# Mixture of experts at the end of a one-core Trainium2 kernel: the table of experts' results laid out by choice, partition and tile, and half-block copies in the last two pairs

## The chip, the cores and the metric

The kernel runs as one program on one core of a Trainium2 chip. The metric is the device time of the whole program in microseconds (us). It computes four layers of attention and feed-forward on the same tokens; the change concerns the last feed-forward layer, a mixture of 64 experts, and above all the last 50 us of the program.

## The reference, cut to what matters

1024 tokens (4 x 256) of width 256. Seven earlier blocks update `x`; the eighth is this one:

```python
def _L3_ffn_ref(hidden_states, gate_w, gate_proj_w, up_proj_w, down_proj_w):
    B, S, H, I, E, K = (2, 128, 256, 96, 64, 8)
    x = hidden_states.reshape(-1, h)
    router_logits = x @ gate_w
    routing_weights, selected = jax.lax.top_k(router_logits, K)
    routing_weights = jax.nn.softmax(routing_weights, axis=-1)
    ...                                   # the 8192 (token, expert) rows sorted by expert
    gate = jax.lax.ragged_dot(hidden_sorted, gate_proj_w, group_sizes)
    up = jax.lax.ragged_dot(hidden_sorted, up_proj_w, group_sizes)
    down = jax.lax.ragged_dot(jax.nn.silu(gate) * up, down_proj_w, group_sizes)
    out = down[unsort].reshape(-1, K, h)
    out = jnp.sum(out * routing_weights[..., None], axis=1)
    return out.reshape(b, s, h)
x = x + _L3_ffn_ref(_layernorm(x), ...)
```

Each token goes to 8 of 64 experts; the 8 results are weighted, summed and added to `x`.

## The kernel before

**Tokens and tiles.** The 1024 tokens are NT = 8 tiles of 128 (P) partitions: token number = tile t x 128 + partition p. Each token has K3 = 8 choices j. Choices are numbered in the order of the experts, so choice 0 of a token is its lowest-numbered expert and choice 7 its highest.

**Tables in device memory.** `hs` holds the experts' inputs: 192 (CAP) rows for each expert. A row is 256 values and one further column, which holds the number of the row of `yd` to which the result belongs. That number is written by the `iota` in `normed_rows` (L1674); unused rows of `hs` hold a number past the end, and the scatter skips them. `yd` has 8192 rows of 256 floats (1 KB each), one for each token and choice: row = token x 8 + choice.

**The experts' loop** (`experts`, L2040) takes two experts (a pair) in each of 32 steps p. Step p computes the gate and up products of pair p (`ps_gu` L2055, `upper_sums` L1982) and the down products of pair p - 1 (`main_sums` L1996, `rest_sums` L2002). The down result `y` has three blocks of 128 rows. Blocks 0 and 2 are complete after `main_sums`; block 1 is half of one expert and half of the other and is made by `rest_sums`. ScalarE copies all three blocks from PSUM to the row buffer `hb` in one instruction (L2083); in the step after the last pair it copies blocks 0 and 2 first (L2079) and block 1 later (L2088). `put_results` (L2007) then has GpSimd issue three indirect DMAs (one for each block, order 0, 2, 1) that scatter the rows to `yd`.

**Loads of results.** `load_results` (L1908) is called from `beside` once all experts that can hold a choice are through: choices 0 and 1 after pair 23, choice 2 after pair 27, 3 after 28, 4 after 29, 5 after 30, and 6 with 7 after pair 31. The SyncE queue (SP) issues these loads in program order, and each waits for the landing of the puts of all pairs up to its own. There are twelve loads, 8 MB in all:

| choices | loads x size | contiguous run in `yd` | order inside a load |
|---|---|---|---|
| 0 and 1 | 2 x 1 MB (tiles 0-3, tiles 4-7) | 2 KB | both choices of a token |
| 2; 3 | 1 x 1 MB each | 1 KB | one choice of all tokens |
| 4; 5 | 2 x 512 KB each (tiles 0-3, 4-7) | 1 KB | one choice |
| 6 and 7 | 4 x 512 KB (two tiles each) | 2 KB | both choices of a token |

The destinations are `deep` and `wt` (choices 0 to 3), `q` and `wmask` (4, 5), `cx` and `ctxT` (6, 7).

**The weighted sums** (`sums`, L2094). Even tiles are summed on TensorE with diagonal weights (`sum_result` L1944), odd tiles on VectorE by multiply-adds into `x` (`add_result` L1939). Four of the VectorE adds are placed beside the last pairs. The other twenty, of choices 1 to 5, wait for `tick`, a GpSimd memset that stands behind the last put (L2101). Then for t = 0, 2, 4, 6: sums of choices 6 and 7 of tile t on TensorE, two adds of tile t + 1 on VectorE, the store of tile t + 1, `add_to_x` of tile t on VectorE (L1779), and its store. The stores go out on ScalarE's queue (L2096).

In this part of the program the order of instructions on each engine is the order written; no scheduler moves them.

Of the kernel before, what the change touches and what calls it, by code (L numbers as in the profile page):

```python
# [23 lines left out]
I32 = mybir.dt.int32  # L24
# [4 lines left out]
P = 128  # L29
B, S, D = 4, 256, 256  # L30
NTOK = B * S
NT = NTOK // P
# [14 lines left out]
E3, I3, K3 = 64, 96, 8  # L47
# [7 lines left out]
LOADS = ((0, 1), (2,), (3,), (4,), (5,), (6, 7))  # L55
# [3 lines left out]
RPP = 2 * CAP // P  # L59
# [57 lines left out]
class Flow:  # L117
# [117 lines left out]
def model(ctx: ExitStack, tc: tile.TileContext, a: dict, out: bass.AP):  # L235
    nc = tc.nc
# [14 lines left out]
    def held(pool, shape, name, dtype=F32):  # L251
        return pool.tile(shape, dtype, tag=name, name=name)
# [4 lines left out]
    def x_t(t):  # L257
        return xb[t // 2][:, t % 2, :]
# [21 lines left out]
    yd = dram.tile([NPAIR, D], F32, tag="yd", name="yd")  # L280

    ctxT = held(early, [P, 2, NTOK], "ctxT")
    cx = held(early, [P, NT, D], "cx")
# [39 lines left out]
        channel_multiplier=-1,  # L323
# [126 lines left out]
    def layers(nk):  # L450
# [41 lines left out]
        def sc(name):  # L492
            return ("sc", [P, 16], name)
# [859 lines left out]
        before = [len(js) for js in puts]  # L1353
# [317 lines left out]
        def normed_rows(t, hx, rows, row_data):  # L1671

            yield Op(POOL, 0.2, (), (hx,))
            nc.gpsimd.iota(  # L1674
                rows[:, :, D : D + 1].bitcast(I32), pattern=[[1, K3], [0, 1]], base=t * P * K3,
                channel_multiplier=K3,
            )
            s = yield Op(DVE, 0.7, (X[t],), new=[sc("st")])
            nc.vector.bn_stats(s[:, 0:6], x_t(t))
            nc.vector.bn_aggr(s[:, 6:8], s[:, 0:6])  # L1680
            nc.vector.tensor_scalar(s[:, 7:8], s[:, 7:8], LN_EPS, None, ALU.add)
            rstd = rstds[:, t : t + 1]
            yield Op(POOL, 0.75, (s,), (s,))
            nc.gpsimd.tensor_tensor(rstd, s[:, 7:8], mhalf, ALU.pow)
            nc.gpsimd.tensor_scalar(s[:, 8:9], s[:, 6:7], rstd, -1.0, ALU.mult, ALU.mult)
            for k in range(2):
                yield Op(ACT, 0.93, (X[t], s, hx), (row_data[k],))
                j = slice(k * K3 // 2, (k + 1) * K3 // 2)
                nc.scalar.activation(
                    rows[:, j, :D], x_t(t).unsqueeze(1).to_broadcast([P, K3 // 2, D]), AF.Identity,  # L1690
                    bias=s[:, 8:9], scale=rstd,
                )
            release(s)
            hx.ready = hx.used = row_data[1].ready
# [131 lines left out]
    with tc.If(rv > 0):  # L1826
# [7 lines left out]
        for t in range(NT):  # L1834
            h = layernorm(t, moe, 1)
# [4 lines left out]
        with tc.For_i(0, E3, 1) as e:  # L1840
# [4 lines left out]
            for c in range(NCH):  # L1845
                pg, pu = ps_mm([I3, CH], "ps_g3"), ps_mm([I3, CH], "ps_u3")
                for ps, o in ((pg, 0), (pu[HALF:], I3), (pu[:HALF], P)):
                    for dc in range(2):
                        at = dc * 2 * I3 + o
# [16 lines left out]
    backs, gats = [], {}  # L1866
    late_rows = [q.bitcast(F32)[:, : NT // 2 * D] for q in (*q2, wmask.rearrange("p t s -> p (t s)"))]
    free_homes = [homes[k % WEIGHTS] for k in range(E3 // GROUP - FIRST, E3 // GROUP - FIRST + 4)]
    n_pairs = E3 // 2

    def choice_weights(t):
# [8 lines left out]
    hbTs, acts, gs = (  # L1880
        [moe_tile(shape, f"{name}{k}", 1) for k in range(2)]
        for name, shape in (
            ("hbT", [P, 2, RPP * P]), ("act", [I3, 2, CAP]), ("g4", [I3, 2, CAP])
        )
    )
# [21 lines left out]

    def load_results(js, p):  # L1908

        half = NT // 2  # L1910
        for h in range(2):
            if js[0] in (0, 2, 3) and (h == 0 or js[0] == 0):
                g = free_homes.pop(0)[:, : NT * D]
            elif js[0] in (4, 5):
                g = late_rows[2 * (js[0] - 4) + h]
            elif js[0] == 6:
                g = (cx.rearrange("p t d -> p (t d)"), ctxT.rearrange("p c r -> p (c r)"))[h]
            else:
                continue
            g = g.rearrange("p (t j d) -> p t j d", j=len(js), d=D)  # L1920
            n = 2 if js[0] == 6 else g.shape[1]
            for j in js:
                gats.setdefault(j, []).append(g)
            for t0 in range(0, g.shape[1], n):
                at = (h * half + t0) * P * K3
                source = yd[at : at + n * P * K3, :].rearrange("(t p j) d -> p t j d", p=P, j=K3)
                ld = nc.sync.dma_start(
                    g[:, t0 : t0 + n].rearrange("p t j d -> p t (j d)"),
                    source[:, :, js[0] : js[-1] + 1, :].rearrange("p t j d -> p t (j d)"),
                )  # L1930
                needs(ld, "back", backs[: RPP * (p + 1)], "results of these choices alone")

    def result(t, j):
        gs = gats[j]
        n = NT // len(gs)
        return gs[t // n][:, t % n, j - min(js for js in LOADS if j in js)[0], :]

    def add_result(t, j):
        return nc.vector.scalar_tensor_tensor(  # L1939
# [56 lines left out]
    def main_sums(act, dn):  # L1996
        y = ps_acc([P, 4, D], "ps_y")
        for i in range(2):
            nc.tensor.matmul(y[:, 2 * i], act[:, i, whole[i]], dn[:, i], start=True, stop=True)  # L1999
        return y  # L2000
# [39 lines left out]
    def experts():  # L2040
        for p in range(in_early - 1, AHEAD - 1):
            load_rows(p)

        nc.scalar.activation(silu, mhalf, AF.Silu)
        nc.vector.tensor_mul(lgs, lgs, wide(kept))
        hbT, turned = rows_turned(0)
        before = ready = None
        for p in range(n_pairs + 1):
            if p < n_pairs:
                e = 2 * p % GROUP  # L2050
                gu, dn = (v[:, e : e + 2] for v in weights[2 * p // GROUP])
                ps = ps_mm([P, 2, CAP], "ps_gu")
                for i in range(2):
                    for dc in range(2):
                        nc.tensor.matmul(  # L2055
                            ps[:, i], gu[:, i, dc, :P], hbT[:, dc, mine[i]], start=dc == 0, stop=dc == 1
                        )
                g = gs[p % 2]
                gated = nc.scalar.activation(g, ps[:I3], AF.Silu)  # L2059
                tc.declare_no_dep(gated.ins, group="gated", reason="ordered through the sums before")  # L2060
                tc.add_to_no_dep_group("gated", gated.ins)
                own = hbT
                act = acts[p % 2]
                if p == 0:
                    ready = upper_sums(p, own, gu, g, act)
                turned = None
                if p + 1 < n_pairs:
                    hbT, turned = rows_turned(p + 1)
                    if p > 0:
                        known(turned, ready)  # L2070
                half = nc.vector.tensor_mul(act[HALF:], ps[I3:], g[HALF:])  # L2071
                product_made(p, half)
            if p > 0:
                yb = hbs[p - 1][:, :, :D]
                y = main_sums(*before)
                if p < n_pairs:
                    ready = upper_sums(p, own, gu, g, act)
                else:
                    nc.scalar.copy(yb[:, ::2, :], y[:, :RPP:2])  # L2079
                mm = rest_sums(y, *before)  # L2080
                if p < n_pairs:
                    known(mm, half)
                    copied = nc.scalar.copy(yb, y[:, :RPP])  # L2083
                    for group in ("back", "rows", "results"):
                        tc.declare_no_dep(copied.ins, group=group, reason="ordered through the rows' use")
                    tc.add_to_no_dep_group("results", copied.ins)
                else:
                    nc.scalar.copy(yb[:, 1, :], y[:, 1])  # L2088
                put_results(p - 1, yb)
                beside(p - 1)  # L2090
            if p < n_pairs:
                before = act, dn
# [120 lines left out]
```

## Time and profile before

| | us |
|---|---|
| median of 4 runs (lowest to highest) | 642.49 (641.33 to 645.07) |
| the profiled execution, its own time | 643.27 |
| its span, first to last instruction | 641.5 |
| mean granted TensorE clock | 0.973 |

| engine | busy us (share of the span) |
|---|---|
| TensorE (PE) | 588.6 (92%) |
| VectorE (DVE) | 424.2 (66%) |
| ScalarE (ACT) | 373.8 (58%) |
| GpSimd (POOL) | 404.0 (63%) |

The experts' loop lies at about 482 to 617 us of the span and what follows it at 617 to 641.5. Times of instructions below are counted from the start of the span. In the lines of a timeline the columns are start, duration (for merged lines, from the first start to the last end), engine, source line, operation, output <- input, count, and in brackets the idle time of the engine before it and what ended it. POOLq, SPq and ACTq are the sequencers of those engines, which issue DMAs. Shares over the whole span say little about this change; it is read from its last 50 us.

### The profile page before, as it was taken

Reading aid. Unit: us, or ns where it says so; the run is one execution under the profiler, and the core shown is the slowest. Engines: PE = TensorE matmul, PEld = TensorE weight load, DVE = VectorE, ACT = ScalarE, POOL = GpSimd, SP = SyncE. Lnnn points to the kernel's source line nnn. Section 1 sums busy time; section 2 is a strip of 40 time slices with the busy share of each in tenths; the row PEclk is TensorE's granted clock in tenths of the full one; section 3 lists DMA queues with packets and bytes.
Section 4 is the critical chain, followed back from the end, with each engine's and each line's share of the span. In section 5 each row is a group of like instructions: output and inputs, shape, how many; then the busy total and the mean of one; then the engine's idle time right before and its main releaser. Section 6 shows DMA issues by size and latency. Waiting matters only on the chain.

```text
span 641.5 us, 10891 instructions
## 1 busy us (share of the span) xinstructions
PE 588.6 (92%) x3727; PEld 450.6 (70%) x3740; DVE 424.2 (66%) x1063; ACT 373.8 (58%) x900; POOL 404.0 (63%) x532
## 2 busy tenths in 40 slices
PE   5997699998999999999999989999739999999995
PEld 4774357686688777877877866886527788778873
DVE  5779947777787789569978757475434555433437
ACT  2233338768888966456886678679434454445420
POOL 6998897132726544664735875787773777676660
PEclk9999899998999999999999989999959999999998
DMA  8999999820210023000003111053458878979687
GB/s 279 363 387 249 212 208 190 269 72 2 83 33 3 1 66 115 2 0 1 1 2 107 42 67 53 31 193 108 156 175 294 263 233 275 308 227 310 211 266 262
DMA packets 66304, 98.12 MB, mean 153 GB/s; under 512 B 7206, under 2 KB 54007, under 8 KB 66240
## 3 DMA queue, kind: packets, MB, share of 16 engines
q1 hardware_dynamic: 56320, 78.40, 42.4%
q0 software_dynamic: 7680, 16.84, 7.4%
q10 hardware_dynamic: 2240, 2.10, 1.0%
q8 instruction: 31, 0.51, 0.4%
q14 instruction: 33, 0.27, 0.1%
HBM read 58.42 MB, written 43.07 MB: 158 GB/s over the span
## 4 chain that ended last, share of the span: by engine, by line
PE 57%; DVE 11%; POOL 10%; ACT 9%; issue 6%; DMA 5%; POOLq 0%; DVEq 0%; SPq 0%; ACTq 0%
PE ps_gu L2055 6%; PE ps_q L1519 5%; PE ps_y L1623 3%; POOL yd L2009 3%; PE ps_u L1986 3%; PE ps_y L1999 3%; PE tp_hb L1892 3%; PE ps_y L1402 2%; POOL hs L1702 2%; PE ps_p L742 2%; PE ps_u L1604 2%; DMA hs<-hx,slots 2%; PE ps_u L1120 2%; PE ps_s L1380 2%; PE tp_q L1277 2%
## 5 line engine op out<-in xcount | busy, mean ns | idle before, releaser
L2009 POOL DMA_INDIRECT yd<-hb x84 | 84.1, 1001 | 34.2 <-issue 20.1
L1702 POOL DMA_INDIRECT hs<-hx,slots x64 | 65.7, 1027 | 24.2 <-issue 13.0
L903 POOL TENSOR_TENSOR st<-st,mhalf 128x1 f32<-128x1 f32 x56 | 33.0, 594 | 57.5 <-DVE st L899 43.5
L1566 ACT ACTIVATE e<-ps_s,nm 128x128 f32<-128x128 f32 x128 | 45.8, 412 | 5.6 <-DVE nm L1560 5.5
L1991 DVE TENSOR_TENSOR act<-ps_u,g 64x192 f32<-64x192 f32 x64 | 22.6, 354 | 39.7 <-PE ps_u L1986 39.3
L2083 ACT COPY hb<-ps_y 128x768 f32<-128x768 f32 x27 | 21.6, 800 | 36.4 <-PE ps_y L2004 36.4
L2071 DVE TENSOR_TENSOR act<-ps_gu,g 32x384 f32<-32x384 f32 x32 | 18.0, 562 | 34.0 <-ACT g L2059 33.8
L1478 POOL TENSOR_TENSOR hh<-g,v 128x512 f32<-128x512 f32 x16 | 20.2, 1273 | 23.8 <-ACT g L1476 20.0
L1281 ACT ACTIVATE qT<-tp_q,rnd 128x512 bf16<-128x512 f32 (+2 forms) x48 | 25.7, 567 | 12.5 <-PE tp_q L1277 12.4
L1566 ACT ACTIVATION_READ_ACCUMULATOR e<-ps_s,nm 128x1 f32 x128 | 31.2, 252 | 0.0
L1533 POOL TENSOR_TENSOR deep<-rt 64x512 f32<-64x512 f32 x20 | 27.3, 1364 | 5.3 <-DVE rt L1529 2.7
L1519 PE MATMUL ps_q<-qc,deep 96*128 96x256 f32 x128 | 30.4, 381 | 0.0
L906 DVE TENSOR_SCALAR h<-x,st 128x256 f32<-128x256 f32 x56 | 27.0, 494 | 5.1 <-POOL st L903 4.8
L1185 ACT ACTIVATE e<-ps_s,nb 128x256 f32<-128x256 f32 x64 | 30.1, 493 | 0.0
L1623 PE MATMUL ps_y<-bo,u 128*128 128x256 f32 x128 | 29.5, 383 | 0.1
L2059 ACT ACTIVATE g<-ps_gu 96x384 f32<-96x384 f32 x32 | 15.6, 486 | 23.2 <-PE ps_gu L2055 23.2
L1900 ACT COPY hbT<-tp_hb 128x768 f32<-128x768 f32 x31 | 24.7, 798 | 7.1 <-PE tp_hb L1892 7.1
L1529 DVE TENSOR_TENSOR rt<-ps_q,rope 128x512 f32<-128x512 f32 x32 | 20.9, 684 | 9.4 <-PE ps_q L1519 9.4
L1583 DVE TENSOR_TENSOR e<-e,nm 128x512 f32<-128x512 f32 x32 | 25.8, 806 | 1.3
L1519 PEld LDWEIGHTS ps_q<-qc,deep 96*128 96x128 f32 x128 | 24.1, 190 | 3.4 <-ACT qc L1505 0.3
L1623 PEld LDWEIGHTS ps_y<-bo,u 128*128 128x128 f32 x128 | 24.0, 193 | 3.4 <-ACT u L1608 0.5
L1120 PE MATMUL ps_g<-hT,w_gate 128*128 128x512 bf16 x69 | 18.6, 406 | 8.3 <-ACT hT L1100 4.5
(373 smaller groups left out, 1778.8 us busy)
## 6 DMA issues: line engine op xcount, KB each, us to landing
hs<-order SPq DMA_DIRECT2D x1, 12336.0 KB
hb<-hs SPq DMA_DIRECT2D x28, 385.5 KB, 5.3
yd<-order SPq DMA_DIRECT2D x1, 8192.0 KB, 31.0
deep<-in_w_gu SPq DMA_DIRECT2D x8, 768.0 KB, 5.8
wt<-in_w_gu SPq DMA_DIRECT2D x6, 768.0 KB, 7.6
deep<-in_w_dn SPq DMA_DIRECT2D x8, 384.0 KB, 6.8
wt<-yd SPq DMA_DIRECT2D x3, 1024.0 KB, 7.1
wt<-in_w_dn SPq DMA_DIRECT2D x6, 384.0 KB, 9.5
```

The costliest lines, as they stand in the source:

```text
L903: nc.gpsimd.tensor_tensor(s[:, 8:9], s[:, 7:8], mhalf, ALU.pow)
L906: nc.vector.tensor_scalar(h[:, k, :], x_t(t), ss[k][:, 6:7], ss[k][:, 8:9], ALU.subtract, ALU.mult)
L1120: nc.tensor.matmul(ps.ap, w[:, dc, o : o + P], q[:, dc, :], start=k == 0, stop=k == n - 1)
L1185: nc.scalar.activation(e[:, mt, :], s[:, mt, :], AF.Exp, bias=nb[:, mt : mt + 1], accum_out=tot[:, 2 * j + mt : 2 * j + mt + 1],)
L1519: nc.tensor.matmul(ps.ap[:, k, :], w[:, hp * P : (hp + 1) * P], qc.ap, start=True, stop=True)
L1533: nc.gpsimd.tensor_add(qv(q[i])[r, hps, :], t0[r], t1[r])
L1566: nc.scalar.activation(wide[:, k, :], s.ap[:, k, :], AF.Exp, bias=nm[:, k : k + 1], accum_out=tot[:, k : k + 1],)
L1583: nc.vector.tensor_mul(wide, wide, tot.unsqueeze(2).to_broadcast([P, n, nk * P]))
L1623: nc.tensor.matmul(y.ap, u[:, hp, :], bo3[:, hp, :], start=hp == 0, stop=hp == H3 // 2 - 1)
L1702: put = nc.gpsimd.indirect_dma_start(out=hs[:, :], out_offset=bass.IndirectOffsetOnAxis(ap=slots[:, t, j : j + 1], axis=0), in_=rows[:, j, ...
L2009: put = nc.gpsimd.indirect_dma_start(out=yd[:, :], out_offset=bass.IndirectOffsetOnAxis(ap=hbs[p][:, j, D : D + 1].bitcast(I32), axis=0), ...
L2055: nc.tensor.matmul(ps[:, i], gu[:, i, dc, :P], hbT[:, dc, mine[i]], start=dc == 0, stop=dc == 1)
```

## The change

1. `yd` gets another order of rows: row = choice x 1024 + p x 8 + t, where it was (t x 128 + p) x 8 + choice. The `iota` that writes the row numbers changes its constants accordingly.
2. `load_results` loads one choice at a time. For a partition, the 8 tiles of one choice now lie side by side. Choices 0 to 3 are one load of 1 MB each, with runs of 8 KB; choices 4 to 7 are two loads of 512 KB each (tiles 0-3, tiles 4-7), with runs of 4 KB. There are again twelve loads with the same bytes. For choices 6 and 7 the order is: 6 of tiles 0-3 (`cx`), 7 of tiles 0-3 (`ctxT`), 6 of tiles 4-7, 7 of tiles 4-7.
3. The results of pair 30 are copied as those of pair 31 were: blocks 0 and 2 in one instruction ahead of `upper_sums` and `rest_sums`, block 1 after them. The first matmul of `rest_sums` then waits for that copy. The copies of pair 31 no longer wait for the landing of earlier puts, a wait that they had and the copies of the other pairs had not.

```diff
-                rows[:, :, D : D + 1].bitcast(I32), pattern=[[1, K3], [0, 1]], base=t * P * K3,
-                channel_multiplier=K3,
+                rows[:, :, D : D + 1].bitcast(I32), pattern=[[NTOK, K3], [0, 1]], base=t,
+                channel_multiplier=NT,
...
     def load_results(js, p):
 
-        half = NT // 2
-        for h in range(2):
-            if js[0] in (0, 2, 3) and (h == 0 or js[0] == 0):
-                g = free_homes.pop(0)[:, : NT * D]
-            elif js[0] in (4, 5):
-                g = late_rows[2 * (js[0] - 4) + h]
-            elif js[0] == 6:
-                g = (cx.rearrange("p t d -> p (t d)"), ctxT.rearrange("p c r -> p (c r)"))[h]
+        for j in js:
+            if j < 4:
+                gats[j] = [free_homes.pop(0)[:, : NT * D]]
+            elif j < 6:
+                gats[j] = late_rows[2 * (j - 4) : 2 * (j - 4) + 2]
             else:
-                continue
-            g = g.rearrange("p (t j d) -> p t j d", j=len(js), d=D)
-            n = 2 if js[0] == 6 else g.shape[1]
+                gats[j] = [(cx.rearrange("p t d -> p (t d)"), ctxT.rearrange("p c r -> p (c r)"))[j - 6]]
+        n = NT if js[0] < 4 else NT // 2
+        for t in range(0, NT, n):
             for j in js:
-                gats.setdefault(j, []).append(g)
-            for t0 in range(0, g.shape[1], n):
-                at = (h * half + t0) * P * K3
-                source = yd[at : at + n * P * K3, :].rearrange("(t p j) d -> p t j d", p=P, j=K3)
-                ld = nc.sync.dma_start(
-                    g[:, t0 : t0 + n].rearrange("p t j d -> p t (j d)"),
-                    source[:, :, js[0] : js[-1] + 1, :].rearrange("p t j d -> p t (j d)"),
-                )
+                source = yd[j * NTOK : (j + 1) * NTOK, :].rearrange("(p t) d -> p (t d)", t=NT)
+                g, at = home_of(t, j)
+                ld = nc.sync.dma_start(g[:, at : at + n * D], source[:, t * D : (t + n) * D])
                 needs(ld, "back", backs[: RPP * (p + 1)], "results of these choices alone")
...
-        before = ready = None
+        before, ready, made = None, None, []
...
                 y = main_sums(*before)
+                steps = (slice(0, RPP, 2), slice(1, 2)) if p >= n_pairs - 1 else (slice(0, RPP),)
+                copies = [nc.scalar.copy(yb[:, k], y[:, k]) for k in steps[:-1]]
                 if p < n_pairs:
                     ready = upper_sums(p, own, gu, g, act)
-                else:
-                    nc.scalar.copy(yb[:, ::2, :], y[:, :RPP:2])
                 mm = rest_sums(y, *before)
                 if p < n_pairs:
                     known(mm, half)
-                    copied = nc.scalar.copy(yb, y[:, :RPP])
+                copies.append(nc.scalar.copy(yb[:, steps[-1]], y[:, steps[-1]]))
+                for copied in copies:
                     for group in ("back", "rows", "results"):
                         tc.declare_no_dep(copied.ins, group=group, reason="ordered through the rows' use")
+                made.append(copies)
+                for copied in made[-3] if len(made) > 2 else ():
                     tc.add_to_no_dep_group("results", copied.ins)
-                else:
-                    nc.scalar.copy(yb[:, 1, :], y[:, 1])
                 put_results(p - 1, yb)
```

More of the change, by code (lines that the diff above doesn't have):

```diff
@@ L1908, in load_results, with home_of @@
     def load_results(js, p):
-        half = NT // 2
-        for h in range(2):
-            if js[0] in (0, 2, 3) and (h == 0 or js[0] == 0):
-                g = free_homes.pop(0)[:, : NT * D]
-            elif js[0] in (4, 5):
-                g = late_rows[2 * (js[0] - 4) + h]
-            elif js[0] == 6:
-                g = (cx.rearrange("p t d -> p (t d)"), ctxT.rearrange("p c r -> p (c r)"))[h]
-            else:
-                continue
-            g = g.rearrange("p (t j d) -> p t j d", j=len(js), d=D)
-            n = 2 if js[0] == 6 else g.shape[1]
+        for j in js:
[3 more added lines that the diff above has]
+                gats[j] = late_rows[2 * (j - 4) : 2 * (j - 4) + 2]
+            else:
+                gats[j] = [(cx.rearrange("p t d -> p (t d)"), ctxT.rearrange("p c r -> p (c r)"))[j - 6]]
+        n = NT if js[0] < 4 else NT // 2
+        for t in range(0, NT, n):
             for j in js:
-                gats.setdefault(j, []).append(g)
-            for t0 in range(0, g.shape[1], n):
-                at = (h * half + t0) * P * K3
-                source = yd[at : at + n * P * K3, :].rearrange("(t p j) d -> p t j d", p=P, j=K3)
-                ld = nc.sync.dma_start(
-                    g[:, t0 : t0 + n].rearrange("p t j d -> p t (j d)"),
-                    source[:, :, js[0] : js[-1] + 1, :].rearrange("p t j d -> p t (j d)"),
-                )
+                source = yd[j * NTOK : (j + 1) * NTOK, :].rearrange("(p t) d -> p (t d)", t=NT)
+                g, at = home_of(t, j)
+                ld = nc.sync.dma_start(g[:, at : at + n * D], source[:, t * D : (t + n) * D])
                 needs(ld, "back", backs[: RPP * (p + 1)], "results of these choices alone")
+    def home_of(t, j):
+        n = NT // len(gats[j])
+        return gats[j][t // n], t % n * D
     def result(t, j):
-        gs = gats[j]
-        n = NT // len(gs)
-        return gs[t // n][:, t % n, j - min(js for js in LOADS if j in js)[0], :]
+        g, at = home_of(t, j)
+        return g[:, at : at + D]
     def add_result(t, j):
```

## The prediction

> **What bounds the kernel now.** I read four views in this order: the chain of waits over the last 50 us, GpSimd's timeline, VectorE's timeline, and the queue of SyncE with the landing times of its loads. First the chain (start, us, what):
>
> ```profile
> 621.26 0.97 POOL yd L2009
> 622.23 0.30 issue
> 622.54 3.60 DMA yd<-hb
> ...
> 626.26 6.68 DMA cx<-yd
> 632.94 0.04 issue
> 632.99 1.15 PE ps_sum L1944 x4
> ...
> 638.17 0.35 DVE x L1779
> ```
>
> The end hangs on GpSimd's last put, then on its landing (3.60 us), then on the first load of choices 6 and 7 (6.68 us), then on the final sums, and VectorE ends at 638.52. The span ends 3.0 us later, after the last store. Why GpSimd is late:
>
> ```profile
> 612.26 0.97 POOL L2009 DMA_INDIRECT yd<-hb  x1 [0.73 <-ACT hb L2083]
> ...
> 616.15 0.97 POOL L2009 DMA_INDIRECT yd<-hb  x1 [0.30 <-issue]
> 617.43 0.97 POOL L2009 DMA_INDIRECT yd<-hb  x1 [0.30 <-issue]
> ...
> 623.50 0.09 POOL L2101 MEMSET tick<- 1x1 f32 x1
> ```
>
> and ScalarE's copies of pairs 30 and 31 beside it:
>
> ```profile
> 614.79 0.80 ACT L2083 COPY hb<-ps_y 128x768 f32<-128x768 f32 x1 [1.65 <-PE ps_y L2004]
> 616.01 0.59 ACT L2079 COPY hb<-ps_y 128x512 f32<-128x512 f32 x1 [0.42 <-DMA yd<-hb]
> 617.35 0.38 ACT L2088 COPY hb<-ps_y 128x256 f32<-128x256 f32 x1 [0.75 <-DMA yd<-hb]
> ```
>
> From 612.26 GpSimd issues nine puts back to back, one every 1.28 us (0.97 + 0.30). Only the first of them waited for ScalarE. The copy of pair 30 was done at 615.59, before its put's turn (616.15); those of pair 31 at 616.60 and 617.73, 3.4 and 2.2 us before theirs (619.98 and later). Now VectorE after `tick`:
>
> ```profile
> 623.62 0.88 DVE L1939 SCALAR_TENSOR_TENSOR x<-deep,choice_w,x 128x256 f32<-128x256 f32 x2 [7.38 <-POOL tick L2101]
> ...
> 630.75 0.88 DVE L1939 SCALAR_TENSOR_TENSOR x<-wmask,choice_w,x 128x256 f32<-128x256 f32 x2
> 633.03 1.00 DVE L1939 SCALAR_TENSOR_TENSOR x<-cx,choice_w,x 128x256 f32<-128x256 f32 x2 [1.41 <-DMA cx<-yd]
> ```
>
> Twenty adds fill 623.62 to 631.63 without a stall (0.40 us each). Then VectorE sits for 1.41 us until the first load of choices 6 and 7 has landed. This 1.41 us is the only slack that faster loads can take out of the end. After it come four rounds of two adds and `add_to_x`, one round every 1.34 us by the starts in the chain (the L1779 rows at 634.15, 635.49, 636.83, 638.17). Last, SyncE's queue:
>
> ```profile
> 617.63 7.79 SPq L1927 DMA_DIRECT2D q<-yd  x3
> 625.46 0.51 SPq L1927 DMA_DIRECT2D wmask<-yd  x1
> 626.26 0.87 SPq L1927 DMA_DIRECT2D cx<-yd  x2
> 627.17 1.07 SPq L1927 DMA_DIRECT2D ctxT<-yd  x2
> ```
>
> The first choice-5 load is the third of the `q` line and is issued at 625.1, when pair 30's puts have landed, although they were issued from 616.15. A put's landing depends on what else the DMA engines carry: from the start of a pair's third put to the release of the load behind it, pair 29 took 2.8 us while one load was only starting, pair 30 took 6.4 us beside 2 MB of choices 3 and 4, and pair 31 took 3.6 us.
>
> **Part 1, the iota.** Other constants, the same instruction and count: nothing. GpSimd's puts have as many rows and the same row length; 1 KB rows go to other places. Put issue takes 0.97 us whatever rows it names (all puts of the loop lie between 0.971 and 1.36 us, the median at 0.973), so 0 for the issue. For the landing I take the bounds 2.8 and 6.4 us above.
>
> **Part 2, the loads.** The same 12 issues on SyncE, the same 8 MB, the same waits; one packet for each run by the counts of this trace (1961 packets for 1.96 MB from 617.6 to 624.5, all 1 KB runs), so 6144 runs become 1536. What a longer run is worth I bound by rows: 1 KB runs and puts together moved 353 GB/s from 617.6 to 624.5; the 2 KB runs with stores moved 356 GB/s from 633 to 637, with slices up to 450. Upper bound 410, the level at which most full slices stop. Lower bound 289 GB/s: the last 3.15 MB, moved from first data at 626.0 to about 636.9. That stretch has a hole around 629 to 631 where the engines were half busy, in runs of 1 and 2 KB. I take 380, between the 2 KB row and the full slices.
>
> [...] The rows do not settle it: 353 at 1 KB includes puts, and nothing here has yet been read from `yd` in 4 KB runs.
>
> Where it counts: choices 0 to 4 have cover. Choices 0 and 1 land at 599.6 and 603.3; VectorE asks for the first at 603.26, TensorE for both from 617.2. Their price without that cover would be the landing itself, 5.4 to 8.6 us. What counts is when the first two loads of choices 6 and 7 land, because now tile 0 needs both (choice 6 of tiles 0-3 and choice 7 of tiles 0-3), where before it needed one. By rate alone, with choice 5 still issued at 625.1 and data from 626.0: 1.05 MB of choice 5 and 1.05 MB of the two loads, 2.1 MB at 380 GB/s = 5.5 us, both landed at 631.5. With choice 5 out of the way earlier (faster choices 3 and 4 release pair 30's puts; the gain is up to 2.4 us, to a landing like pair 31's): pair 31's landing at 626.1, data 0.9 us later, 1.05 MB at 380 = 2.8 us, landed at 629.8. So both are there between 629.8 and 631.5, and VectorE's adds end at 631.63. TensorE, which needs 1.13 us for a tile's last four matmul passes, follows within the 1.34 of VectorE's round. The third and fourth load come 1.3 to 2.8 us after, by 634.3, when tile 4's round is due (631.66 + 2 x 1.34).
>
> The end then is set by VectorE: 631.66 + 4 x 1.34 = 637.0 where it was 638.52. This is 1.5 us less, and it is a ceiling too: the adds wait for `tick` at 623.5, which stands behind GpSimd's row of puts that no part of the change shortens. At 353 GB/s and choice 5 at 625.1, the loads land at 631.95, which leaves 1.2. At 289 GB/s they land at 633.3, and the end moves later by 0.4.
>
> **Part 3, the copies.** One more ScalarE instruction; 0.59 + 0.38 instead of 0.80 for pair 30. The first part can start when `main_sums` end (613.48 + 0.09, the gap of pair 31), and ends at 614.16, 1.4 us before the old copy. GpSimd is at pair 29's puts until 615.85, so this brings 0. If GpSimd were free it would bring up to 1.4 us. The new wait: `rest_sums` of pair 30 on TensorE starts at about 614.21 instead of 614.11; behind it in TensorE's order stand `main_sums` of pair 31 at 614.82 and the sums at 617.2. Up to 0.1 us, under the same cover of GpSimd's queue. The waits of pair 31's copies (0.42 and 0.75 us) go away; GpSimd is next late there too, so 0. Bounds for part 3: -0.05 (the seam at 616.15, where one issue took 1.33 instead of 1.28) and +0.1. I take 0.
>
> **Sum.** -1.5 on the profiled execution: 643.27 to 641.8, span 641.5 to 640.0. The profiled time stands 0.78 above the median; on the median the forecast is 642.49 - 1.5 = 641.0.
>
> **Rivals.**
> A, the other side: a longer run is worth nothing, and the first round waits for two loads. The first two loads of `cx` land 1.33 us apart before (TensorE got them at 632.99 and 634.32). If the first still lands at 632.94, tile 0 starts at 634.3 instead of 633.03, and with the last load two tiles remain instead of one: +1.3 us, 643.8. It decides from the point where the second load lands later than 633.1. For it: the rate before was no steadier than 289 over that stretch. Against it: a quarter of the runs, and the stretch's hole lies where many short runs queue.
> [...]
> [...]
> C: nothing is won, because the loads ahead only move the hole (choice 4's load, released at 617.6 beside an idle DMA, now competes with choice 3's): within 0.4 us of before, 642.5.
>
> **How the numbers follow.** Forecast 0.58 (640.5 to 641.9), A 0.17 (642.8 to 643.9), B 0.10 (642.0 to 646.5), C 0.15. 0.5% is 3.2 us, about what a measurement of this kernel can tell from no change, and the runs before span 0.6% themselves. Forecast, A, C and the near half of B lie inside it. Faster by more needs something beyond the ceiling of 1.5, or the spread of the runs: 0.11. Slower by more is the far half of B and the same spread: 0.09. The range takes the forecast with the runs' own lower spread (642.49 - 641.33 = 1.2, so 641.0 - 1.4 = 639.6) up to A's end, 644.0; the far part of B is left out.
>
> **What would show it.** Right: `cx` and `ctxT` have both landed before 631.7, VectorE goes from the `wmask` adds to the `cx` adds without a wait, ends at about 637.0, and GpSimd's nine puts stand at the same times as before. Wrong: VectorE still waits for `cx` or `ctxT` (A or B; B if the `cx` issue comes later than 626.3), or GpSimd's last put starts at another time than 622.5, which would mean that the copies or the puts themselves do count.

## The result and the profile after: slower by 0.28%

| | before | changed |
|---|---|---|
| median us (lowest to highest) | 642.87 (639.74 to 647.18, 67 runs) | 644.75 (641.84 to 647.89, 41 runs) |
| profiled execution, its own time | 643.27 | 644.08 |
| its span | 641.5 | 642.2 |
| granted TensorE clock, mean | 0.973 | 0.971 |

The ratio is 1.0028, interval 1.0019 to 1.0038: about 1.8 us lost where 1.5 us of gain was forecast. The time lies above the range.

The two profiles can't be laid over each other by the clock on the wall: the experts' loop stands 1.68 us earlier in the changed kernel's (the last put starts at 620.86, before at 622.54). The change moves nothing ahead of the loop but the constants of an iota, and further profiles of both tables on chips of this speed have that put anywhere from 620.9 to 623.3. The prediction named another start than 622.5 as a sign that the copies or the puts count; with this spread, and with the same spacing of the puts, it is no sure sign of that. So I count from the start of the last put. From there to the end of the span before takes 18.96 us (641.5 - 622.54) and the changed kernel 21.34: the tail grew by 2.4 us.

VectorE's timeline of the changed kernel, the rows that answer to those shown of before:

```profile
621.92 4.84 DVE L1934 SCALAR_TENSOR_TENSOR x<-wt,choice_w,x 128x256 f32<-128x256 f32 x12 [7.36 <-POOL tick L2097]
...
629.05 0.88 DVE L1934 SCALAR_TENSOR_TENSOR x<-wmask,choice_w,x 128x256 f32<-128x256 f32 x2
631.88 0.48 DVE L1934 SCALAR_TENSOR_TENSOR x<-cx,choice_w,x 128x256 f32<-128x256 f32 x1 [1.96 <-DMA cx<-yd]
633.34 0.48 DVE L1934 SCALAR_TENSOR_TENSOR x<-ctxT,choice_w,x 128x256 f32<-128x256 f32 x1 [0.97 <-DMA ctxT<-yd]
634.61 0.42 DVE L1779 TENSOR_TENSOR x<-ps_sum,x 128x256 f32<-128x256 f32 x1 [0.79 <-PE ps_sum L1939]
...
636.32 0.42 DVE L1779 TENSOR_TENSOR x<-ps_sum,x 128x256 f32<-128x256 f32 x1 [0.37 <-PE ps_sum L1939]
```

The twenty adds are where they were (9.1 us after the last put's start, both kernels). Before, one wait of 1.41 us followed. Now four follow: 1.96 for the load of choice 6, 0.97 for that of choice 7, and 0.79 and 0.37 for TensorE, 4.09 in all. That is 2.68 more than before, where the end came 2.40 later, partly because the last two rounds take 1.25 us instead of 1.34. So these waits are the loss that the profile shows, and each has its own reason. The chain shows the first two:

```profile
620.86 6.08 DMA yd<-hb
...
627.06 0.32 SPq L1922
627.38 0.04 issue
627.43 5.82 DMA ctxT<-yd
633.25 0.14 issue
633.38 2.91 PE ps_sum L1939 x6
```

The last puts land after 6.08 us (before 3.60), and the second load of the first round 5.82 us after its issue. SyncE's queue tells why the landing is late:

```profile
618.33 1.53 SPq L1922 DMA_DIRECT2D q<-yd  x3
619.90 0.55 SPq L1922 DMA_DIRECT2D wmask<-yd  x1
```

Choice 5's loads went out at 619.5 and 619.9, ahead of pair 31's last put; before, they went out 2.6 and 2.9 us behind it. GpSimd's nine puts stand 1.28 us apart as before (610.58 to 620.86), so the copies moved nothing there. For TensorE, the table by stretches (columns: stretch, length, busy time and count for PE, PEld, DVE, ACT, POOL, then granted clock, DMA share, GB/s):

```profile
628.00:630.00 2.00, 0.44 (x3) 0.03 (x1) 1.93 (x5) 0.00 (x0) 0.00 (x0) 0.97 0.98 240
630.00:632.00 2.00, 0.17 (x1) 0.17 (x2) 0.12 (x1) 0.00 (x0) 0.00 (x0) 0.50 0.92 236
632.00:634.00 2.00, 1.67 (x4) 0.90 (x5) 0.85 (x2) 0.00 (x0) 0.00 (x0) 0.50 1.02 401
634.00:636.00 2.00, 2.00 (x6) 1.63 (x5) 1.30 (x3) 0.00 (x0) 0.00 (x0) 0.50 0.64 246
```

TensorE had idled for 3.40 us before the sums of choice 6, the granted clock fell to 0.50, and the sums of the first two tiles and part of the third ran at that. A tile's four passes, 1.13 us before, then take 1.7 us, more than VectorE's round of 1.34. The last tile runs at full speed again (granted clock 1.00 from 637). The last column shows the loads at 236 to 240 GB/s in their first four us and at 401 after that. The same table of the kernel before:

```profile
628.00:630.00 2.00, 1.05 (x3) 0.87 (x4) 2.00 (x7) 0.00 (x0) 0.00 (x0) 0.69 0.97 316
630.00:632.00 2.00, 2.00 (x6) 1.64 (x5) 1.63 (x5) 0.00 (x0) 0.00 (x0) 0.50 0.90 288
632.00:634.00 2.00, 1.53 (x6) 0.69 (x5) 0.93 (x2) 0.00 (x0) 0.00 (x0) 0.96 1.05 387
```

The clock had fallen to 0.50 there too, in a wait of 1.98 us (from 626.97 to 628.95). But it rose again before the final sums began at 632.99, and VectorE was busy with its twenty adds meanwhile. So it is not the slow clock that is new, but that it lies under the final sums.

### The profile page after: what moved, and what is told of

Its sections match the earlier page's. It is cut to its first block, busy times and chain, and to the rows that moved or that the text cites. A ratio compares the mean times of both kernels' runs of the same rounds, so it can differ in the third digit from the quotient of the medians.

```text
span 642.2 us, 10890 instructions
## 1 busy us (share of the span) xinstructions
PE 588.7 (92%) x3727; PEld 449.5 (70%) x3740; DVE 423.5 (66%) x1063; ACT 374.0 (58%) x901; POOL 403.8 (63%) x532
## 4 chain that ended last, share of the span: by engine, by line
PE 60%; DVE 10%; ACT 9%; POOL 9%; issue 5%; DMA 5%; POOLq 0%; DVEq 0%; SPq 0%; ACTq 0%
PE ps_gu L2050 7%; PE ps_q L1519 5%; PE ps_y L1994 4%; PE ps_u L1981 3%; POOL hs L1702 3%; PE tp_hb L1892 3%; PE ps_g L1120 3%; PE ps_u L1120 2%; PE ps_y L1623 2%; PE ps_y L1402 2%; PE ps_p L742 2%; POOL yd L2004 2%; PE ps_y L1999 2%; DMA hs<-hx,slots 2%; PE ps_s L1380 2%
## 5 line engine op out<-in xcount | busy, mean ns | idle before, releaser
L2078 ACT COPY hb<-ps_y 128x768 f32<-128x768 f32 (+1 forms) x28 | 21.6, 770 | 36.3 <-PE ps_y L1999 36.3
L1478 POOL TENSOR_TENSOR hh<-g,v 128x512 f32<-128x512 f32 x16 | 20.2, 1274 | 23.8 <-ACT g L1476 19.9
L1120 PE MATMUL ps_g<-hT,w_gate 128*128 128x512 bf16 x69 | 20.1, 431 | 7.7 <-ACT hT L1100 4.3
L1529 DVE TENSOR_TENSOR rt<-ps_q,rope 128x512 f32<-128x512 f32 x32 | 20.9, 684 | 9.4 <-PE ps_q L1519 9.4
```

The lines of the kernel that those rows point to most:

```text
L1120: nc.tensor.matmul(ps.ap, w[:, dc, o : o + P], q[:, dc, :], start=k == 0, stop=k == n - 1)
```

## The experiments

They ran on several chips, on which the kernel before takes from 642.6 to 681.6 us; every ratio is against the kernel before on the same chip. On the slow chips the intervals are 0.2 to 0.4% to each side, about as wide as the loss. So I read the profiles as well, in us from the start of the last put: when the first load of choices 6 and 7 is issued (it waits for the last landing), when VectorE ends, and when the span ends (the tail).

| kernel | ratio (interval) | first issue | VectorE ends | tail |
|---|---|---|---|---|
| before, first profile | | 3.7 | 16.0 | 19.0 |
| before_again | 1.0007 (0.9970 to 1.0045) | 5.1 | 15.5 | 18.5 |
| changed, first profile | 1.0028 (1.0019 to 1.0038) | 6.2 | 18.4 | 21.3 |
| after_again | 1.0037 (1.0009 to 1.0065) | 5.7 | 18.1 | 21.0 |
| e1_copies_only | 1.0031 (1.0003 to 1.0058) | 6.5 | 16.6 | 19.6 |
| e1_again | 1.0016 (0.9993 to 1.0040) | 5.7 | 16.3 | 19.2 |
| e2_layout_only | 1.0023 (0.9996 to 1.0051) | 7.2 | 20.1 | 24.5 |
| e3_hold5 | 1.0001 (0.9973 to 1.0030) | 4.5 (choice 5 first, 3.6) | 17.1 | 20.0 |
| e5_short_runs | 0.9998 (0.9973 to 1.0023) | 5.7 | 17.1 | 20.2 |
| c1_hold3 | 1.0058 (1.0022 to 1.0093) | 5.3 | 18.3 | 21.3 |
| c2_hold3_both | 1.0044 (1.0012 to 1.0075) | 5.4 | 17.9 | 20.9 |
| e4_both_choices | 1.0021 (1.0003 to 1.0040) | 6.2 | 17.7 | 20.7 |
| e6_pe_filled | 1.0015 (0.9996 to 1.0034) | 6.3 | 17.7 | 21.0 |
| e7_homes_swapped | 1.0023 (1.0004 to 1.0042) | 5.9 | 18.1 | 21.1 |
| d1_both_filled | 1.0006 (0.9990 to 1.0023) | 6.6 | 17.0 | 19.9 |
| f1_pitch9 | 0.9986 (0.9965 to 1.0006) | 3.5 | 15.9 | 19.0 |
| f2_pitch9_both_filled | 1.0039 (1.0017 to 1.0060) | 2.5 | 18.1 | 21.1 |
| f3_short_two_tiles_filled | 1.0029 (1.0002 to 1.0056) | 5.4 | 18.1 | 21.4 |
| g1_pitch9_both | 1.0006 (0.9989 to 1.0024) | 6.8 | 17.6 | 20.6 |
| g2_before_pitch9 | 0.9994 (0.9976 to 1.0012) | 6.7 | 16.1 | 19.0 |

**First set: the two parts, the landing, the length of a run.** One kernel takes the copies alone, one the table and loads alone:

> The kernel before with the copies of pairs 30 and 31 alone changed; yd and the loads as before. All theories of the slowdown (T: choice 5's load gets ahead of the last puts; R: long runs hold up the puts; W: the new order of rows makes the scatter's writes land later) blame the table, so all expect no effect: ratio 1.000 +- 0.001 to before. Counted from the start of GpSimd's last put, the times of before should come back: landing (SyncE's release) +3.6 us, end of the span +19.0. If the copies or the waits taken from them do matter, the nine last puts will no longer stand 1.28 us apart or the end will lie beyond 19.0 +- 0.4.

> The changed kernel with the old copies: table, loads and their order changed alone. T, R and W expect the whole loss here: ratio 1.002 to 1.004 to before, last landing +6.1 us, end of the span +21.3 us after the start of the last put. If the copies took part, the ratio would lie nearer to 1.000 or above 1.004.

The profiles put the loss into the table: with the old table VectorE ends at 16.3 to 16.6, with the new one at 20.1. (e2's last stores, at 4.4 us behind VectorE against 2.9 to 3.3 elsewhere, also came late; I have no reason for that.) The copies were run again later:

> The kernel before with the changed copies alone, once more, since its first interval (1.0003 to 1.0058) just left out 1. If the copies cost nothing, 0.999 to 1.001 and a tail of 18.5 to 19.6; if they cost what that interval says, above 1.001.

With 1.0031 and 1.0016 their ratios lie above 1, and their tails 0.5 to 0.9 us above the mean of before's two profiles. Weighted by their intervals, the two ratios give 1.0022 (1.0004 to 1.0040, an estimate from both), as much as the 1.0023 of the table alone. So the times of the whole program can't tell the two parts of the change apart; only the tails do. The nine puts stand as expected, so nothing that the copies were priced at shows; whether they cost a tenth or two of a per cent elsewhere is left open.

What e1 did show was unexpected. SyncE's queue, with the old table:

```profile
657.69 0.51 SPq L1927 DMA_DIRECT2D wmask<-yd  x1
664.35 0.87 SPq L1927 DMA_DIRECT2D cx<-yd  x2
```

Its last put started at 657.81. Choice 5's loads went out ahead of it, and the landing came 6.5 us after it, as in the changed kernel, but without its loss. Next, choice 5 held back in the changed kernel:

```diff
-        loaded[last] = js
+        loaded.setdefault(n_pairs - 1 if js == (5,) else last, []).append(js)
```

> The changed kernel, with the two loads of choice 5 held back until pair 31's puts have landed; they then stand ahead of the loads of choices 6 and 7 in SyncE's queue. T: with 1 MB less in flight beside the last puts they land 3.0 to 4.0 us after the last put's start instead of 6.1; the first two loads of choices 6 and 7 then come after 2.1 MB, at about +3.5 +0.9 +2.1 MB at 0.38 MB/us (5.5) = +9.9 instead of +12.4, and the end at about +19.5 instead of +21.3: ratio about 1.000 to 1.001 to before. R: choice 4's load of 4 KB runs is still in flight, so the landing comes at about +5. W: the landing stays near +6.1, since the rows written are the same; the end then lies later than in the changed kernel (more bytes after the landing), +23.

The landing came at 3.6 instead of 6.2, as the theory of the load in flight says. Half of the loss stayed: VectorE ended at 17.1, since choice 5 and the two loads of the first round now came in a row. Not all of the other half need be the landing, since TensorE's slow stretch (granted clock 0.50, about 662 to 665 in e3's profile) now lay ahead of the final sums. Last in this set, runs of 1 KB with the same twelve loads:

```diff
-                ... pattern=[[NTOK, K3], [0, 1]], base=t, channel_multiplier=NT,
+                ... pattern=[[NTOK, K3], [0, 1]], base=t * P, channel_multiplier=1,
-                source = yd[...].rearrange("(p t) d -> p (t d)", t=NT)
+                source = yd[...].rearrange("(t p) d -> p t d", p=P)
```

> The changed kernel with rows of yd numbered choice x 1024 + tile x 128 + partition: the same twelve loads of one choice each in the same order, but in runs of 1 KB. R: with short packets the last landing comes back to about +3.6 us. T: what counts is whether choice 5's load is issued ahead of the last puts' landing; where it is, the landing stays at 5 to 6.5 us, where choices 3 and 4 are slow enough that it is not (as in before), the landing is +3.6 and choice 5 lies behind. W: other rows than in either kernel, so nothing definite. For the end, T and R both expect more than before by about 1.3 us for the first round that needs two loads: ratio 1.001 to 1.004.

With short packets in flight the puts land as late as with long ones (first issue at 5.7, against 6.2 and 5.7 in the changed kernel's two profiles), so a packet's length is not the reason. VectorE ended 1.0 to 1.3 us earlier than in the changed kernel.

**Second set: is the late landing a race, and is it the loss?**

> The kernel before, unchanged, for a second profile. The theory by now (G): a put lands only when the 1 MB load that got in flight ahead of it has drained, so which pair's puts land early is a close race between them and the loads that they release. In before's profile pair 29 just won (2.8 us from its third put's start to SyncE's release) against choice 3's load, so choices 3 and 4 were in flight together, pair 30 lost (6.4), choice 5 was issued late and pair 31 landed after 3.6. G allows both patterns here: pair 31 at about 3 to 4 us with choice 5 issued after +2 us from the last put's start and the end at about +19.0, or, where pair 29 loses (5 us or more), choice 5 issued before +0.5, pair 31 at 6 to 6.6 us and the end at about +19.5. The rival (L: only the new table does this) expects the first pattern alone.

> The changed kernel, unchanged, on this chip. G: choice 3's load is issued earlier against pair 29's last put than in before, so pair 29 loses nearly always: pair 31's landing 6 to 7.3 us, end +20 to +21.5, ratio 1.002 to 1.004. L expects the same.

Before falls in both patterns: here it issued its last choice-5 load 0.1 us after the last put's start, landed at 5.1, and still had the shortest tail of all, 18.5. In the five profiles with the old order of rows (g2, below, among them) the first issue lies at 3.7, 5.1, 5.7, 6.5 and 6.7, and VectorE ends at 15.5 to 16.6 whichever it is. So the late landing alone is not the loss: where choice 5 is ahead of the puts, it is no longer ahead of the last loads. TensorE's slow clock alone is not the loss either: in before_again it idled 3.41 us before the final sums, ran the first of them at half clock (0.50) and cost VectorE one wait of 1.06. Then choice 3 was held until pair 29 had landed:

```diff
+        loaded.setdefault(29 if js == (3,) else last, []).append(js)
```

> The changed kernel with choice 3's load held until pair 29's puts have landed (it then goes out with choice 4's). G: nothing is in flight beside pair 29's puts, which land after 2.6 to 3.3 us; choices 3 and 4 go out together, pair 30 lands late behind them (5 us or more), choice 5 is issued after +1 us from the last put's start, and pair 31 lands after 3 to 4.5 us, as in before's first profile; the end comes 1 to 2 us earlier than in the changed kernel, at +19 to +20. L (long runs or the new rows are slow in themselves): pair 31 still lands after 6 us and the end stays at +21.

> As the run with choice 3 held, and the last four loads take two tiles of both choices each (runs of 2 KB), so that the first round waits for one load and not two. G: a further 1.3 us earlier, the end at +17.5 to +19; ratio to before 0.998 to 1.000. If the loads of 4 KB runs were slow by their length, the gain is larger, up to 2.5 us; if the wait for two loads costs nothing, the end is as in the run before.

Neither came out as expected, and their ratios are the highest of the table. Choice 5 was issued 3.5 us after the last put's start, so the landing order was that of before, but the landing took 5.3 and VectorE now waited 1.2 us for choice 5. In these two, holding a load only moved the wait. Over all twenty profiles, the first issue came 5.1 to 7.2 us after the last put's start in the fourteen where a load of choice 5 was out before that start. Where choice 5 came later it was 2.5 to 3.7 (before, f1, f2, and choice 5's own in e3), or 5.3 and 5.4 (c1, c2, where choices 3 and 4 went out together).

**Third set: the waits on VectorE's timeline, one by one.** e4 gives the first round one load again, with the loads of before:

```diff
+        if js[0] == 6:
+            for t in range(0, NT, 2):
+                source = yd[6 * NTOK :, :].rearrange("(j p t) d -> p j (t d)", p=P, t=NT)
+                ...   # two tiles of both choices into cx (tiles 0-3) or ctxT (tiles 4-7)
```

e6 puts six products that nothing reads between the sums of choices 5 and 6:

```diff
+        for _ in range(6):
+            nc.tensor.matmul(tp_rows[:, 0, :D], diag[:, 0, 0, :], result(0, 0), start=True, stop=True)
```

d1 has both, and e7 exchanges the destinations of choices 4 and 5 with those of 6 and 7.

> The changed kernel, with the last four loads taking two tiles of both choices each (2 KB runs), as in before; table, runs of choices 0 to 5 and copies stay changed. Theory by now (M): of the 2.4 us that the tail grew, little is the landing, most is the wait of the first round for two loads that come 1.5 to 1.9 us apart, and the slow TensorE clock after that longer idle time. M expects: the last landing stays late (5 to 6.5 us after the last put's start), but VectorE goes from its first cx add to its end in 5.5 to 6.2 us instead of 7.4 to 7.8, and the tail (last put's start to the end of the span) is 18.5 to 19.7 us as in before, against 21.0 to 21.3; ratio 0.999 to 1.001. The rival (P: the late landing of the puts is the loss) expects the tail to stay above 20.5 and the ratio at 1.002 to 1.004.

> The changed kernel with six further products of the same shape (0.56 us each, into a PSUM tile that nothing reads any more) on TensorE between the sums of choice 5 and those of choice 6, so that it doesn't idle there. If the slow clock of the last sums (1.06 us for two passes of matmul instead of 0.59) comes from that idle time, the rounds take 1.34 us again instead of 1.7 and the tail shrinks by 0.7 to 1.1 us, to 19.9 to 20.5: ratio 1.001 to 1.003. If the clock has nothing to do with it, or VectorE is the bound anyway, the tail stays at 21.0 to 21.3.

> Both remedies in the changed kernel: the last four loads of two tiles of both choices, and the six products that keep TensorE busy. M expects the shortest tail, 17.8 to 19.0 us, and a ratio of 0.997 to 1.000; if the late landing is the loss, still above 20.

> The changed kernel with the homes of choices 4 and 5 exchanged with those of 6 and 7 (same source, same runs of 4 KB, same order). The last loads moved at only 213 to 250 GB/s in their first 4 us, and choices 4 and 5 at about 400 with the same runs. If the destination does it, choices 6 and 7 now come at 350 to 400 and choices 4 and 5 slower, the second load lands about 1.5 us earlier after its issue (4.5 instead of 5.9 to 6.2), and the tail is 19.5 to 20. If it is the source (rows written just before) or the start of any run of loads, nothing changes: tail 21.0 to 21.3, ratio 1.002 to 1.004.

Neither remedy alone is worth more than 0.3 to 0.7 us by VectorE's end, because the next wait takes its place. In e4 VectorE starts tile 0 with one load, and then waits 0.85 us for a slow TensorE. In e6 the clock holds at 1.00 and the rounds take 1.3 us, but the second load came 1.85 us after the first. Both together bring the ratio to 1.0006 and VectorE's end to 17.0; the ratios of the three have intervals that overlap, so it is the profiles that part them. VectorE's rows of d1 show rounds without a wait for TensorE:

```profile
634.70 1.01 DVE L1945 SCALAR_TENSOR_TENSOR x<-cx,choice_w,x 128x256 f32<-128x256 f32 x2 [2.35 <-DMA cx<-yd]
635.82 0.42 DVE L1779 TENSOR_TENSOR x<-ps_sum,x 128x256 f32<-128x256 f32 x1
...
637.14 0.42 DVE L1779 TENSOR_TENSOR x<-ps_sum,x 128x256 f32<-128x256 f32 x1
```

What is left of the loss in d1 is that 2.35, where before had 1.41. e7 left everything as it was (tail 21.1, and 209 to 250 GB/s from 2.2 to 5.2 us after the first issue): the destination is not what makes the last loads slow.

**Fourth and fifth set: the slow start of the last loads.** With one unused row behind each eight, partitions' rows lie 9 KB apart:

```diff
+PT = NT + 1
+NPAIR = P * PT * K3
-                ... pattern=[[NTOK, K3], [0, 1]], base=t, channel_multiplier=NT,
+                ... pattern=[[P * PT, K3], [0, 1]], base=t, channel_multiplier=PT,
```

> The changed kernel with one unused row behind each eight of yd, so that a partition's rows start 9 KB apart and not 8 KB (row = choice x 1152 + p x 9 + t); runs and order of loads as in the changed kernel. The last loads began at 200 to 280 GB/s for 4 us with runs of 2 and 4 KB at a pitch of 8 KB, wherever they went to, and at 350 to 373 with 1 KB runs at a pitch of 1 KB. If the pitch does it (the engines' streams meet in the same part of the memory), they now begin at 350 or more, the second load lands 4.5 us after the first issue instead of 6.2, and the tail is about 19.5 to 20. If it is something else (run length, or rows just written), they begin at 200 to 280 again and the tail is 20.7 to 21.3. The table's fill with zeros, early in the program, is an eighth longer, up to 3 us of transfers that lie beside other work.

> The same 9 KB pitch with the last four loads of two tiles of both choices, and the six products that keep TensorE busy. If the pitch matters, each round waits for little and the tail is 18 to 19, ratio 0.997 to 1.000; if not, as the run with both remedies and 8 KB pitch: 19.5 to 20, ratio 0.999 to 1.002.

> The changed kernel with rows choice x 1024 + tile x 128 + p (1 KB runs), the last loads two tiles of one choice each (eight of 256 KB, so that a round waits for 512 KB), and the six products. If what counts are the first round's bytes, the clock and the start of the last loads, this has all three put right, with the landing still late: the second of the eight loads lands about 3.5 us after the first issue, and the tail is 18 to 19 us, ratio 0.997 to 0.999. If eight issues of 0.5 us each on SyncE hold the loads up, the later rounds wait and the tail is 19 to 20.

> The 9 KB pitch with the last four loads of two tiles of both choices, without the six products (which were 4 us of work on TensorE's path once the loads came early). If pitch and the first round's bytes are the two causes, VectorE goes from the adds of choice 5 to those of 6 and 7 without a wait, 9.0 us after the last put's start, and ends 5.4 to 6.0 later: tail 17.4 to 18.3, against 18.5 to 19.0 of before; ratio 0.996 to 0.999. If the pitch was only luck of one profile, the loads begin at 200 to 280 GB/s again and the tail is above 19.5.

> The kernel before with the 9 KB pitch alone: row = token x 9 + choice; runs, loads and copies as before. If the pitch is a cause by itself, the last loads and those of 1 KB runs both move at 340 to 400 GB/s, and the tail is 17.5 to 18.5; ratio 0.997 to 1.000. If it matters only for the long runs of the changed table, tail and ratio are those of before: 18.5 to 19.5, 0.999 to 1.001.

The mean GB/s from 3 to 5 us after the first issue of the last loads, in the fourteen profiles where choice 5 was out before the last put: 223 to 245 in six of seven profiles of the changed table at 8 KB (the changed kernel twice, e2, e4, e6, e7; d1, with e4's loads, 350), with the DMA engines busy for 83 to 94% of the time in the six. With 9 KB it is 410 and 401 (g1, g2). With 1 KB runs it is 362 in e5, but 215 in f3. And it is 367 to 381 in before_again, e1 and e1_again, whose pitch is 8 KB too. (f1 and f2, with 9 KB, moved 336 and 301, but their last loads followed choice 5 without a pause.) So among the fourteen 9 KB goes with fast loads, and slow ones are found in new tables only. Pitch by itself is not the cause, and what it is in the new table stays open.

f1 lost nothing against before (0.9986), but it also landed early (3.5), so its 15.9 is not owed to the rate alone. f2 and f3 miss their numbers for a reason of mine: their loads were there 9 us after the last put's start, when VectorE asked for them, and the six products were then 2.8 to 4.0 us of work ahead of the final sums. f2's VectorE timeline:

```profile
674.17 0.42 DVE L1780 TENSOR_TENSOR x<-ps_sum,x 128x256 f32<-128x256 f32 x1 [3.93 <-PE ps_sum L1951]
```

g1 has the fast rate, one load for the first round and no filler, and missed too: it landed at 6.8, TensorE had idled 2.69 us, and its clock was 0.50:

```profile
632.00:634.00 2.00, 2.00 (x6) 1.59 (x5) 0.94 (x3) 0.00 (x0) 0.00 (x0) 0.50 1.06 405
```

g2, with an idle time of 2.14 us and the same landing, kept a clock of 1.00 and ended VectorE at 16.1 instead of 17.6:

```profile
632.00:634.00 2.00, 1.78 (x8) 0.90 (x6) 1.81 (x5) 0.00 (x0) 0.00 (x0) 1.00 1.03 396
```

No version was shown to beat the kernel before: the lowest ratios, 0.9986 and 0.9994, have intervals that hold 1.

## Why the prediction was wrong

- **What bounds the tail** was read rightly: GpSimd's nine puts at 1.28 us, the landing, the last loads, VectorE's rounds. The puts, the copies' cover and the twenty adds stand as forecast. The ceiling of 1.5 was not quite one: the wait to be won was 1.41 us, and four rounds had taken 5.49 (633.03 to 638.52) where 4 x 1.34 makes 5.36, which gives 1.4; where nothing held the rounds up, they took 1.25 each (f1, f2). For the same reason the 0.4 of loss at 289 GB/s comes out as 0.1 to 0.3. And a ceiling was the wrong thing to take for the likeliest value.
- **The landing of pair 31, taken at 3.6 us, was 6.1.** The prediction saw that choice 5's loads could be released earlier, and booked that as a gain only. Released earlier, they were in flight ahead of the last put. B, with its 0.10 for 642.0 to 646.5, stands for puts held up by the length of the loads' runs, which no run shows: with 1 KB runs the landing was much the same (5.7 in e5), and with choice 5 held it was 3.6 (e3). The 3.6 also came from one profile that turned out to be the exception: the four later ones with the old order of rows have 5.1 to 6.7, so faster loads need not have been what released choice 5. By itself this term cost little with the old order of rows, where VectorE's end hardly moved with it.
- **From the first issue to both loads of the first round: 3.7 us forecast (0.9 + 2.8 at 380 GB/s), 6.2 measured** (627.06 to 633.25). This is the term that failed most plainly: with it and the landing, both loads were there 12.4 us after the last put's start, where 7.3 to 9.0 was forecast and the adds end at 9.1. The rate was taken from stretches in which the loads were already running; these moved 236 to 240 GB/s for four us. The lower bound of 289 was an average over a slow part and a fast one, and the first round stands in the slow part. The prediction put the dip at 629 to 631 in before's own trace down to short runs; with runs of 4 KB it was there again, and longer.
- **Rival A's mechanism was there**: the second load came 1.46 us after the first by VectorE's rows, where A had 1.33. It was priced as an alternative to the forecast, given too little chance, and had no term for what follows. Its 1.3 us of loss lie below the 1.8 measured.
- **TensorE, said to "follow within the 1.34 of VectorE's round", did not.** This term was missing: its idle time before the `cx` sums grew from 0.47 us to 3.40, the final sums fell into a slow stretch of the clock (0.50 granted), and 0.79 + 0.37 us of waits followed. In e6, where TensorE was kept busy, these two were 0.26 and nothing. How long a wait it takes is not settled by the profiles: the clock was at 0.50 after 1.98 us in before, 2.69 in g1 and 3.40 in the changed kernel, and still at 1.00 after 2.14 in g2.
- **Length of a run.** Once the last loads ran (5 to 7 us after their first issue), 1 KB runs moved 351 GB/s in e5 and 4 KB runs 395 and 401 in the changed kernel's two profiles. So a longer run was worth something there, and 380 was no bad running rate; the first round did not get to it.
- **The copies** were priced at 0 and moved none of GpSimd's puts; two ratios above 1 (1.0022 together) leave a cost open that the ratios can't tell from the table's.

## What to carry to other kernels

A load that is released earlier is also in flight earlier: ask which puts it now stands in front of, and don't book the release as a gain until that is answered. When loads are regrouped, count what the first consumer needs before it can start, not the bytes in all; and price the first of them by the slow stretch that the trace shows, not by the running rate (here 236 to 240 GB/s against 401). When a wait on the path grows, look at who idles beside it: here TensorE came back at a granted clock of 0.50 after waits of 1.98, 2.69 and 3.40 us. And take a second profile before a single landing time goes into a sum: here the one at hand was the exception.

## What the runs showed of the hardware

- Put landing went with the loads in flight and not with the length of their packets: 2.5 to 7.2 us for the same last put, late with either table (6.5 in e1 with the old order of rows, 7.2 in e2 with the new), and late with runs of 1 KB (5.7 in e5) and of 4 KB (6.2 in the changed kernel).
- The granted TensorE clock fell to 0.50 in waits of 1.98 (before), 2.69 (g1) and 3.40 us (the changed kernel), and stayed at 1.00 through one of 2.14 (g2), so the length of the wait alone doesn't decide it. Every slow stretch seen whole in the last 31 us of the twenty profiles lasted 3.41, 6.83 or 10.24 us (added up from windows of half a microsecond), multiples of one length. In before it lasted 3.41 us, in the changed kernel 6.82.
- The last loads moved 207 to 294 GB/s from 1 to 3 us after their first issue in all fourteen profiles where choice 5 was out before the last put, and 341 to 401 from 5 to 7 us. How long the slow start lasts differs: from 3 to 5 us it was still 223 to 245 in six of seven profiles of the changed table at 8 KB, and 367 to 381 in before_again, e1 and e1_again. A slow stretch of two us (188 to 279 GB/s by half microseconds, 629.26 to 631.26) lies in the middle of before's last loads too, where choice 5's were just ahead, so a pause isn't needed for it. The reason is not settled.
- Chips differ: the kernel before took 642.6, 643.3, 673.9, 675.0 and 681.6 us (medians) on five of them.
